# First propagation step of a four-layer graph network: two neighbouring pairs at once, with the operands swapped, against one pair at a time

## The chip, the cores and the metric

The kernel runs on one core of one Trainium2 chip, in one launch. The metric is the device time of that launch in microseconds (us). Everything is float32, and all four layers of the network, both steps of the last one included, are in this single program.

## The reference

Four layers work on 3327 nodes with 256 features each, every layer behind a layer norm and a ReLU, with a residual. Only the fourth is touched. In it `X` is the normed input, `S` the adjacency matrix, and two steps run, each with a sparse attention matrix `A` made from the current `Xa`:

```python
R = S + eye(N); R = R / R.sum(-1, keepdims=True)
Z, Xf, Xa = 0, X, X
for n in range(2):
    A  = top_p_attention(Xa, W1, W2, W3)   # softmax rows, cut to 90% of their mass
    Xf = R @ Xf                            # "propagation"
    Xa = A @ Xa
    Z  = Z + Xf @ U1[n].T + Xa @ U2[n].T
h = X + Z
x = x + layernorm(h)
```

What matters here is the first step's `R @ X`, a product of a 3327 x 3327 with a 3327 x 256 matrix, and what becomes of its result: it is multiplied by `U1[0].T` for `Z`, and it is the `Xf` of the second step.

## The kernel before

The nodes are 26 blocks of 128 rows (`T = 26`, `P = 128`); two blocks `p` and `p + 13` form a pair (`H = 13`). The product with `R` uses a scheme with seven products in place of eight on half matrices (numbers 1 to 7 in the code): sums of the adjacency's quarters, made in the third layer, lie in `s_dram`, and sums of the features' quarters in `ts`. So the first step costs 13 pairs x 7 products x 13 blocks of 128 x 128 x 128. `load_now` (L1255) loads a *slab*, 13 blocks of one product's adjacency operand (832 KB), through SP's queue into one of three buffers, and for four of the seven products GpSimd adds the identity to one block of it (L1264).

`PropagatedPair.steps` (L1272) issues the products: the slab's block is the stationary operand of TensorE, 128 feature columns are the moving one (L1295). A pair has two phases (`PHASES`: products 1, 2, 5, 4 and then 6, 7, 3; pair 0 has `FIRST_PHASES`). Their results collect in two PSUM banks; `half` (L1301) copies the first to SBUF on ScalarE, `whole` (L1306) adds the second in with VectorE. The results have nodes on the partitions.

`PropagationOfFirstStep` (L1356) then takes each block of 128 nodes: `scale` divides by the row sums on ScalarE, `turn` transposes the block with two TensorE transposes (L162, tile `pt_f`) and a ScalarE copy, and `sums` (L1372) multiplies by U1. It uses that the first step's share of `Z` can be folded into the second step: `sums` computes X U1[0] + Xf U1[1] with four matmuls of 256 columns (tiles `hT`, the turned input, loaded back from `hT_dram`, and `xT_f`), and this sum is what the second step multiplies by `R`. It is stored in `fs_dram` and read back as `fs` before the second step.

TensorE's order is written by hand (`manual_schedule(engines=PE_ALONE)`); the other engines' orders come from a scheduler. In the first step, row block `m` of the attention matrix goes through these stations: logits (L1063) and exponentials (L1088) three blocks ahead (`AHEAD = 3`), two ScalarE passes, then a search on VectorE that ends in the selection L1166; then TensorE turns the 26 blocks of the row (L202), ScalarE copies them (L205), and TensorE multiplies them by the features (L213). Between two row blocks TensorE runs one phase of a propagation (`propagate_first`), but for the row blocks in `APART = (3, 7, 11, 15, 19)`. The first `EARLY = 4` phases run before row block 0, the last three phases (`T - 3` to `T - 1`) follow row block 25 and lead to the second step. `plan` dictionaries say after which unit of a phase another piece of work (logits, `turn`, `sums`, `rows.begin` of the next row) is put into TensorE's order.

Of the kernel before, what the change touches and what calls it, by code (L numbers as in the profile page):

```python
# [11 lines left out]
F32 = mybir.dt.float32  # L12
# [35 lines left out]
def kernel(  # L48
# [73 lines left out]
    hT_dram = dram.tile([P, T, NC, P], F32, name="hT_dram")  # L122
    fs_dram = dram.tile([P, T, D], F32, name="fs_dram")
# [33 lines left out]

    def transposed(src, pool, name):

        pt = ps_tr.tile([P, 4, P], F32, tag="tr", name=f"pt_{name}")  # L160
        for c in range(NC):
            nc.tensor.transpose(pt[:, c, :], src[:, c * P : (c + 1) * P], ident)  # L162
        dst = pool.tile([P, NC, P], F32, tag="xT", name=f"xT_{name}")
        last_copied.append(nc.scalar.copy(dst, pt[:, :NC, :]))
        return dst
# [126 lines left out]
    def layers_0_to_2(again):  # L292
# [141 lines left out]
        class Pair:  # L434
# [27 lines left out]
            def turn(self):  # L462
                self.xT = turn_pair(self.xn, AF.Copy if self.layer == 3 else AF.Relu, *self.pool, self.name)
                if self.layer == 3:
                    for i in range(2):
                        nc.scalar.dma_start(hT_dram[:, self.p + i * H], self.xT[:, :, i * P : (i + 1) * P])
# [531 lines left out]
    def layer_3_in(again, tag, big, ep, w3, sm3, h3, kT0, ksum0, left):  # L998
# [16 lines left out]
        u1s = big.tile([P, 2, NC, D], F32, name="u1s")  # L1015
# [3 lines left out]
        def constants():  # L1019
            nc.scalar.dma_start(u1s, u1t.rearrange("s (c p) e -> p s c e", p=P))  # L1020
            for i in range(2):
                nc.scalar.dma_start(u2s[:, :, i, :], u2t[i].rearrange("(c p) e -> p c e", p=P))
# [69 lines left out]
        def search_steps(step, m, e, parts, st, dens, alone):  # L1092
# [49 lines left out]
            below, first, cand = s("below", 4), s("first"), s("cand", 8 * T)  # L1142
# [11 lines left out]
            for k in range(ROUNDS):  # L1154
                nc.vector.max(v[:, 8 * k : 8 * k + 8], cand)
                if k + 1 < ROUNDS:
                    left = s(f"cand{k % 2}", 8 * T)
                    nc.vector.match_replace(left, v[:, 8 * k : 8 * k + 8], cand, 0.0)
                    cand = left
# [51 lines left out]
        def propagated_steps(acc, step, m, xf):  # L1211
# [3 lines left out]
            for n, k in enumerate(order):  # L1215
                g, j = k // H, k % H
                if g not in slab:
                    s = slab[g] = slabs.tile([P, H, P], F32, tag="slab", name=f"slab3{tag}_{step}_{m}_{g}")
# [8 lines left out]
        FIRST_PHASES = (1, 2, 3), (5, 7, 4, 6)  # L1227
        PLACE3 = {2: (0, 0), 1: (0, 1), 4: (0, 2), 5: (0, 3), 6: (1, 0), 7: (1, 1), 3: (1, 2)}

        def combining(h, ts, a, b):  # L1230
# [5 lines left out]
            yield nc.vector.tensor_tensor(t3, part(1, 1), part(0, 1), ALU.subtract)  # L1236
            yield nc.vector.tensor_tensor(t2, part(1, 1), t1, ALU.subtract)
            yield nc.vector.tensor_tensor(t4, part(1, 0), t2, ALU.subtract)

        def combine(h, ts, a, b):  # L1240
            run(combining(h, ts, a, b))

        class PropagatedPair:


            def __init__(self, step, p, h, ts):
                self.step, self.p, self.h, self.ts = step, p, h, ts
                self.accs, self.slabs, self.name = {}, {}, f"{step}{tag}_{p}"
                self.last = step == 1 and p == H - 1

            def load(self, n):
                with tc.issue_after(slabs_behind[-1].ins) if slabs_behind else nullcontext():
                    self.load_now(n)

            def load_now(self, n):  # L1255
                p = self.p
                x = self.slabs[n] = slabs.tile([P, H, P], F32, tag="slab", name=f"slab3{tag}_{self.step}_{p}_{n}")
                if n in (1, 2, 4):
                    i, j = {1: (0, 0), 2: (0, 1), 4: (1, 1)}[n]
                    self.loaded = nc.sync.dma_start(x, adj_t[p + i * H, :, j * H : (j + 1) * H, :])  # L1260
                else:
                    self.loaded = nc.sync.dma_start(x, s_dram[:, p, {5: 0, 6: 1, 7: 2, 3: 3}[n]])
                if n in (1, 4, 5, 7):
                    added.append(nc.gpsimd.tensor_tensor(x[:, p, :], x[:, p, :], ident, ALU.add))  # L1264

            def right(self, n, k):
                if n in (1, 2, 3):
                    i, j = {1: (0, 0), 2: (1, 0), 3: (1, 1)}[n]
                    return self.h[:, i * H + k, j * P : (j + 1) * P]
                return self.ts[:, {5: 0, 6: 1, 7: 2, 4: 3}[n], k, :]  # L1270

            def steps(self, phase):  # L1272

                first = self.p == 0
                ns = (FIRST_PHASES if first else PHASES)[phase]
                units = [(n, k) for n in ns for k in range(H)]
                if first and not phase:
                    units.sort(key=lambda u: u[1] == H - 1)
                if first and not phase:
                    ends = w3.tile([P, 4, P], F32, tag="eT", name="ends", bufs=3)  # L1280
                    for i, n in enumerate(ns):
                        nc.sync.dma_start(ends[:, i, :], adj_t[0, :, n * H - 1, :] if n < 3 else s_dram[:, 0, 3, H - 1])
                place = {**PLACE3, 3: (2, 0)} if self.last else PLACE3
                last = {place[n][0]: (n, k) for n, k in units} if phase or not first else {}
                for at, (n, k) in enumerate(units):
# [6 lines left out]
                    a = self.slabs[n][:, k, :]  # L1292
                    if first and not phase and k == H - 1:
                        a = ends[:, ns.index(n), :]
                    nc.tensor.matmul(  # L1295
                        self.accs[bank][:, c * P : (c + 1) * P], a, self.right(n, k),
                        start=start, stop=last.get(bank) == (n, k), skip_group_check=True,
# [3 lines left out]
            def half(self):  # L1301
                self.y = w3.tile([P, 4, P], F32, tag="xf", name=f"xf_{self.name}")
# [53 lines left out]
        class PropagationOfFirstStep:  # L1356


            def __init__(self, m, rows):
                self.m, self.xf = m, rows  # L1360
                self.hT = w3.tile([P, NC, P], F32, tag="hT", name=f"hT_{m}")
                nc.sync.dma_start(self.hT, hT_dram[:, m])

            def scale(self, behind=last_turned):
                with tc.issue_after(behind[-1].ins):
                    nc.scalar.activation(self.xf, self.xf, AF.Copy, scale=rinv[:, self.m : self.m + 1])

            def turn(self):
                with tc.high_priority():
                    self.xT = transposed(self.xf, w3, f"f_{self.m}")  # L1370

            def sums(self):  # L1372
                acc = one_bank(f"u1_{self.m}")
                parts = [(xT[:, c, :], u1s[:, s, c, :]) for s, xT in enumerate((self.hT, self.xT)) for c in range(NC)]
                for i, (xT, u) in enumerate(parts):
                    nc.tensor.matmul(acc[:, :D], xT, u, start=(i == 0), stop=(i == len(parts) - 1))
                last = self.m % H == H - 1
                rows = fs[0][:, self.m, :] if last else self.hT.rearrange("p c n -> p (c n)")
                with tc.high_priority():
                    nc.scalar.copy(rows, acc[:, :D])  # L1380
                if not last:
                    nc.sync.dma_start(fs_dram[:, self.m, :], rows)

        def finish3(m, y, rows, name, behind=None):
# [3 lines left out]
            x3 = w3.tile([P, NC, P], F32, tag="hT", name=f"x3_{name}").rearrange("p c n -> p (c n)")  # L1388
            with tc.issue_after(behind.ins) if behind else nullcontext():
                nc.sync.dma_start(z, z_dram[:, m, :])  # L1390
                nc.sync.dma_start(x3, x3_dram[:, m, :])
# [26 lines left out]
        def finish_last(m, y, rows, acc, name, behind):  # L1418

            z = w3.tile([P, D], F32, tag="z", name=f"z1_{name}")  # L1420
            x3 = w3.tile([P, NC, P], F32, tag="hT", name=f"x3_{name}").rearrange("p c n -> p (c n)")
            with tc.issue_after(behind.ins):
                nc.sync.dma_start(z, z_dram[:, m, :])
                nc.sync.dma_start(x3, x3_dram[:, m, :])
# [18 lines left out]
        def finish_pair(p, both, pair):  # L1443
# [4 lines left out]
            zs, xs = [], []  # L1448
            for i in range(2):
                m = p + i * H  # L1450
                zs.append(w3.tile([P, D], F32, tag="z", name=f"z1_{m}"))
                xs.append(w3.tile([P, NC, P], F32, tag="hT", name=f"x3_{m}").rearrange("p c n -> p (c n)"))
                with tc.issue_after(pair.loaded.ins):
                    nc.sync.dma_start(zs[i], z_dram[:, m, :])
                    nc.sync.dma_start(xs[i], x3_dram[:, m, :])
                nc.gpsimd.tensor_tensor(zs[i], zs[i], ys.pop(m), ALU.add)
# [8 lines left out]
            for i in range(2):  # L1465
                z, x3, m = zs[i], xs[i], p + i * H
# [20 lines left out]
        def queries(step, m, name):  # L1487
            if step:
                return qT[:, m * P : (m + 1) * P]
            q = w3.tile([P, NC, P], F32, tag="xT", name=f"q_{name}")[:, 0, :]  # L1490
# [110 lines left out]
        APART = (3, 7, 11, 15, 19)  # L1601
# [4 lines left out]
        with tc.manual_schedule(engines=PE_ALONE):  # L1606
# [38 lines left out]
            pairs, fs = {}, []  # L1645

            def propagate_first(n, at):

                p, phase = divmod(n, 2)
                pair = pairs.setdefault(p, PropagatedPair(0, p, h3, ts))  # L1650
                units = H * len((PHASES if p else FIRST_PHASES)[phase])
                run(pair.steps(phase), {int(k * units // T): v for k, v in at.items()})
                if phase == (p == 0):
                    pair.half()
                if phase and n != T - 3 and n != T - 1:
                    rows_of_first(p)

            def rows_of_first(p):
                rows = pairs.pop(p).whole()
                for i in range(2):  # L1660
# [305 lines left out]
```

## Time and profile before

| | us |
|---|---|
| three timed runs, median (lowest to highest) | 2505.57 (2505.36 to 2507.46) |
| the profiled execution | 2506.95 |
| its span, first to last instruction | 2505.2 |
| TensorE busy in the span | 2484.1 (99%) |
| VectorE busy | 2093.6 (84%) |
| ScalarE busy | 1085.2 (43%) |
| GpSimd busy | 298.4 (12%) |

The first step of layer 3 lies between about 937 us (first propagation product) and 1781 us (first turning of the second step); the second step follows until the end. In the profile a float32 matmul shows as two records of TensorE, a transpose of a block as one. A line such as `L1295 PE MATMUL f0a<-h3a,slab3a 128*128 128x128 f32 x1008` names the program line, the engine, the operation, what is written from what, the stationary operand's size, the moving operand's size and type, and the number of records. In a timeline the first column is the start in us from the span's start, the second the length; the lengths of pipelined matmuls overlap, so the spacing of starts tells what one costs. Square brackets show how long the engine had been idle before, and what ended it. The granted clock of TensorE was 0.998 of full speed over the span.

### The profile page before, as it was taken

How to read it: one execution, taken by the hardware profiler on the slowest of the kernel's cores; microseconds unless marked ns; L12 is line 12 of the kernel's file. 1: busy time of each engine (PE TensorE's matmuls, PEld its weight loads, DVE VectorE, ACT ScalarE, POOL GpSimd, SP SyncE). 2: the span in 40 equal slices, each digit the busy share in tenths (PEclk: the TensorE clock that was granted, in tenths of full speed). 3: DMA queues.
4: the chain of work that ended last, by engine and by line, in shares of the span. 5: the costliest groups of instructions: out<-in, count | busy, mean ns of one | idle time of the engine just before them, and what ended most of it. 6: DMA issues, size and time to landing. Idle time of an engine off the chain costs nothing. (4 is left out here: it accounts for less than half of the span.)

```text
span 2505.2 us, 47792 instructions
## 1 busy us (share of the span) xinstructions
PE 2484.1 (99%) x17967; PEld 2256.5 (90%) x17967; DVE 2093.6 (84%) x5536; ACT 1085.2 (43%) x2158; POOL 298.4 (12%) x462
## 2 busy tenths in 40 slices
PE   9999999999999999999999999999999999999998
PEld 8999999999999998888888888888888888888887
DVE  7876789899887778788879797884999999999995
ACT  3101034443111115565656565653655655555551
POOL 2000010000000001000000000000121222322221
PEclk9999999999999999999999999999999999999999
DMA  6777766555798867323132323133433343344333
GB/s 201 228 232 240 225 192 185 174 178 177 240 315 285 281 210 227 96 81 108 58 121 80 110 85 106 57 108 113 164 122 109 109 138 121 109 129 140 124 110 114
DMA packets 181773, 388.28 MB, mean 155 GB/s; under 512 B 19741, under 2 KB 78746, under 8 KB 181530
## 3 DMA queue, kind: packets, MB, share of 16 engines
q1 hardware_dynamic: 153210, 364.31, 45.1%
q10 hardware_dynamic: 28320, 20.80, 2.6%
q8 instruction: 143, 2.34, 0.4%
q14 instruction: 100, 0.82, 0.1%
HBM read 315.44 MB, written 67.89 MB: 153 GB/s over the span
## 5 line engine op out<-in xcount | busy, mean ns | idle before, releaser
L205 ACT COPY eT_a<-pt_a 128x512 f32<-128x512 f32 (+1 forms) x364 | 196.4, 554 | 379.1 <-PE pt_a L202 376.7
L213 PE MATMUL a<-h3a,eT_a 128*128 128x256 f32 x1352 | 323.2, 382 | 0.0
L213 PE MATMUL a<-vs,eT_a 128*128 128x256 f32 x1352 | 320.3, 382 | 0.2 <-ACT eT_a L205 0.2
L1150 DVE MAX8 cand_a<-w 128x8 f32<-128x128 f32 x1352 | 288.4, 278 | 4.3
L213 PEld LDWEIGHTS a<-h3a,eT_a 128*128 128x128 f32 x1352 | 244.8, 190 | 33.3 <-ACT eT_a L205 2.1
L213 PEld LDWEIGHTS a<-vs,eT_a 128*128 128x128 f32 x1352 | 245.3, 191 | 29.9 <-ACT eT_a L205 0.7
L603 PE MATMUL acc_a<-tsa,s_a 128*128 128x128 f32 (+1 forms) x2028 | 269.9, 275 | 0.0
L603 PE MATMUL acc_a<-tsa,a_a 128*128 128x128 f32 x2028 | 251.6, 275 | 0.0
L603 PEld LDWEIGHTS acc_a<-tsa,s_a 128*128 128x128 f32 x2028 | 248.8, 192 | 0.7
L603 PE MATMUL acc_a<-rhs,a_a 128*128 128x128 f32 (+1 forms) x2028 | 248.6, 276 | 0.0
L603 PEld LDWEIGHTS acc_a<-tsa,a_a 128*128 128x128 f32 x2028 | 239.6, 192 | 0.5
L603 PEld LDWEIGHTS acc_a<-rhs,a_a 128*128 128x128 f32 x2028 | 236.7, 192 | 0.6
L1146 DVE SCALAR_TENSOR_TENSOR w<-e_a,t_a 128x896 f32<-128x896 f32 x208 | 225.5, 1084 | 3.0
L1264 POOL TENSOR_TENSOR slab3a<-slab3a,ident 128x128 f32<-128x128 f32 x100 | 114.3, 1143 | 912.6 <-DMA slab3a<-in_adj_t_dram 348.7
L202 PE MATMUL pt_a<-ident,e_a 128*128 128x128 f32 x1352 | 199.7, 274 | 3.0 <-DVE e_a L1166 2.8
L1088 ACT ACTIVATE e_a<-pl_a 128x1024 f32<-128x1024 f32 x260 | 184.5, 728 | 36.9 <-PE pl_a L1063 35.4
L202 PEld LDWEIGHTS pt_a<-ident,e_a 128*128 128x128 f32 x1352 | 166.2, 141 | 32.4 <-DVE e_a L1166 2.7
L1137 DVE SCALAR_TENSOR_TENSOR w<-e_a,t_a 128x3328 uint8<-128x3328 f32 x52 | 191.6, 3684 | 4.3
L1166 DVE SCALAR_TENSOR_TENSOR e_a<-e_a,all_least 128x3328 f32<-128x3328 f32 x52 | 191.9, 3690 | 1.8
L755 ACT ACTIVATE a_a<-a_a 128x640 f32<-128x640 f32 (+1 forms) x156 | 101.6, 666 | 163.0 <-DVE a_a L753 130.9
L420 ACT ACTIVATE xT_a<-pt_a 128x512 f32<-128x512 f32 x52 | 30.8, 593 | 321.1 <-PE pt_a L416 282.1
L1295 PE MATMUL f0a<-tsa,slab3a 128*128 128x128 f32 x1352 | 167.7, 276 | 0.0
(265 smaller groups left out, 4215.3 us busy)
## 6 DMA issues: line engine op xcount, KB each, us to landing
slab3a<-s_dram SPq DMA_DIRECT2D x100, 832.0 KB, 4.5
a_a<-in_adj_t_dram SPq DMA_DIRECT2D x312, 256.0 KB, 4.1
slab3a<-in_adj_t_dram SPq DMA_DIRECT2D x79, 832.0 KB, 4.6
a_a<-in_adj_t_dram SPq DMA_DIRECT2D x156, 320.0 KB, 4.0
s_dram<-s_a SPq DMA_DIRECT2D x78, 256.0 KB, 5.1
s_dram<-s_a SPq DMA_DIRECT2D x39, 320.0 KB, 4.5
x_dram<-x_a ACTq DMA_DIRECT2D x39, 256.0 KB, 3.7
s_dram<-a_a SPq DMA_DIRECT2D x26, 256.0 KB, 5.1
```

The lines of the kernel that those rows point to most:

```text
L202: nc.tensor.transpose(pt[:, j, :], e[:, k * P : (k + 1) * P], ident)
L205: last_turned.append(nc.scalar.copy(eT[:, : len(blocks), :], pt[:, : len(blocks), :]))
L213: nc.tensor.matmul(acc[:, :width], ready[g][:, j, :], rhs[:, k, :], start=(k == 0), stop=(k == T - 1))
L603: nc.tensor.matmul(self.acc[:, g, at : at + wide], quads[n][:, k - CUTS[c][0], :], t, start=(k == 0 and n in (1, 4)), stop=(k == H - 1 and ...
L755: nc.scalar.activation(a, a, AF.Tanh)
L1088: last_exp.append(nc.scalar.activation(dst, src, AF.Exp, accum_out=parts[:, c : c + 1]))
L1137: nc.vector.scalar_tensor_tensor(junk, e, t, e, ALU.is_lt, ALU.mult, accum_out=got)
L1146: nc.vector.scalar_tensor_tensor(w[:, : (b - a) * P], eg, t, eg, ALU.is_lt, ALU.mult, accum_out=below[:, g : g + 1])
L1150: nc.vector.max(cand[:, 8 * k : 8 * k + 8], w[:, (k - a) * P : (k - a + 1) * P])
L1166: nc.vector.scalar_tensor_tensor(e, e, least, e, ALU.is_ge, ALU.mult, accum_out=st["kept"][:, m : m + 1])
L1264: added.append(nc.gpsimd.tensor_tensor(x[:, p, :], x[:, p, :], ident, ALU.add))
L1295: nc.tensor.matmul(self.accs[bank][:, c * P : (c + 1) * P], a, self.right(n, k), start=start, stop=last.get(bank) == (n, k), skip_group_ch ...
```

## The change

The first step takes two neighbouring pairs, `p` and `p + 1`, at once (six doubles and one single pair 12), and the operands are swapped: 128 feature columns are stationary, and the blocks of both pairs' slabs, 256 columns, are moving. The results so come out turned, features on the partitions. The transposes, the scaling before them and `hT` go. The turned block is the stationary operand of one product with both U1[0] and U1[1] side by side (512 columns); the division by the row sums is done when that result is copied from PSUM. The half with U1[1] is read back as `fs` (so `fs` no longer holds the input's share), and the half with U1[0] is kept in `u_dram` and added to `z` by GpSimd in the second step. A double has four phases; its slabs come in pieces of 6 + 6 + 1 blocks per product, the last blocks of a phase's products sharing one buffer. The plans and `APART` are set anew.

```diff
-    hT_dram = dram.tile([P, T, NC, P], F32, name="hT_dram")
-    fs_dram = dram.tile([P, T, D], F32, name="fs_dram")
+    u_dram = dram.tile([P, T, 2, D], F32, name="u_dram")
...
+        OF_DOUBLE = (1, 2), (5, 4), (6, 3), (7,)
+        OF_LAST_DOUBLE = (1, 2), (5, 4), (6,), (3, 7)
+        OF_SINGLE = (1, 2, 5, 4), (6, 3, 7)
+        DOUBLES = H // 2
...
+        def load_slab(dst, n, p, q, a, b):
+            loaded = nc.sync.dma_start(dst, slab_source(n, p, q, a, b))
+            if n in (1, 4, 5, 7):
+                for t in range(p, q):
+                    if a <= t < b:
+                        x = dst[:, t - p, t - a, :]
+                        added.append(nc.gpsimd.tensor_tensor(x, x, ident, ALU.add))
+            return loaded
...
+        class FirstPropagation:
+            def __init__(self, d):
...
+                self.cuts = (0, H) if self.many == 1 else (0, 6, 12, H)
...
+            def units(self, phase):
+                units = [(n, k) for n in self.phases[phase] for k in range(H)]
+                if self.many > 1:
+                    units.sort(key=lambda u: u[1] == H - 1)
+                return units
+            def steps(self, phase):
...
+                for at, (n, k) in enumerate(units):
+                    c = sum(k >= b for b in self.cuts[1:-1])
+                    if (n, c) not in self.slabs:
+                        self.load(phase, n, c)
+                    nc.tensor.matmul(
+                        self.acc[:, self.at[n]], right_half(h3, ts, n, k), self.slabs[n, c][:, :, k - self.cuts[c], :],
+                        start=not at, stop=at == len(units) - 1, skip_group_check=True,
+                    )
+                    yield at
+            def keep(self, phase):
...
+                        nc.scalar.copy(
+                            y, self.acc[:, k * width : (k + 2) * width].rearrange("p (n f) -> p n f", n=2)
+                        )
...
+                        if n == 6:
+                            nc.vector.tensor_tensor(y0[:, 0:1, :], y0[:, 0:1, :], y0[:, 1:2, :], ALU.add)
+                            nc.vector.tensor_tensor(y0[:, 1:2, :], y0[:, 1:2, :], b, ALU.add)
+                            nc.vector.tensor_tensor(y1, y1, both(y0[:, 1:2, :]), ALU.add)
+                        elif n == 3:
+                            nc.vector.tensor_tensor(y0[:, 1:2, :], y1[:, 1:2, :], b, ALU.add)
+                        else:
+                            nc.vector.tensor_tensor(y1, y1, both(b), ALU.add)
...
         class PropagationOfFirstStep:
-            def __init__(self, m, rows):
-                self.m, self.xf = m, rows
-                self.hT = w3.tile([P, NC, P], F32, tag="hT", name=f"hT_{m}")
-                nc.sync.dma_start(self.hT, hT_dram[:, m])
-            def scale(self, behind=last_turned):
-                with tc.issue_after(behind[-1].ins):
-                    nc.scalar.activation(self.xf, self.xf, AF.Copy, scale=rinv[:, self.m : self.m + 1])
-            def turn(self):
-                with tc.high_priority():
-                    self.xT = transposed(self.xf, w3, f"f_{self.m}")
+            def __init__(self, m, yT):
+                self.m, self.yT = m, yT
             def sums(self):
-                acc = one_bank(f"u1_{self.m}")
-                parts = [(xT[:, c, :], u1s[:, s, c, :]) for s, xT in enumerate((self.hT, self.xT)) for c in range(NC)]
-                for i, (xT, u) in enumerate(parts):
-                    nc.tensor.matmul(acc[:, :D], xT, u, start=(i == 0), stop=(i == len(parts) - 1))
+                m, acc = self.m, one_bank(f"u1_{self.m}")
+                for c in range(NC):
+                    nc.tensor.matmul(
+                        acc, self.yT[:, c, :], u1s[:, c].rearrange("p s e -> p (s e)"),
+                        start=(c == 0), stop=(c == NC - 1),
+                    )
+                rows = w3.tile([P, 2, D], F32, tag="rows", name=f"u1_{m}", bufs=1)
...
+                        nc.scalar.activation(rows.rearrange("p s e -> p (s e)"), acc, AF.Copy, scale=by)
...
+                    nc.sync.dma_start(u_dram[:, m], rows)
...
         def finish3(m, y, rows, name, behind=None, of_pair=None):
...
+            nc.gpsimd.tensor_tensor(z, z, u, ALU.add)
             nc.gpsimd.tensor_tensor(z, z, y, ALU.add)
...
-        APART = (3, 7, 11, 15, 19)
+        APART = (2, 6, 11, 16, 21)
...
-                    propagate_first(0, dict(zip((23, 25.4), ([what] for what in left.stages))))
+                    propagate_first(0, dict(zip((15, 18, 19, 22), ([what] for what in (*left.stages, sum_keys, centre_keys)))))
...
-                    steps = prepare(0, 0, kT0)
-                    centred = {7.5: [lambda: centre(kT0, mean0(), "0"), lambda: next(sums_of_first)]}
-                    propagate_first(1, merged(centred, whole_run(steps, 14.5), plan))
+                    propagate_first(1, merged(whole_run(prepare(0, 0, kT0), 3), {12: [lambda: next(sums_of_first)]}))
...
-                    steps = prepare(0, m + AHEAD, kT0)
-                    after = {3: [a.turn], 15: [a.node], 18: [a.values], 20: [lambda: rows.begin(m + 1)]}
-                    propagate_first(next(propagated), merged(whole_run(steps, 10), after, later))
+                    steps, n = prepare(0, m + AHEAD, kT0), next(propagated)
+                    at = (4, 14, 18, 22, 24) if n % 4 == 3 else (3, 10, 15, 18, 20)
+                    what = a.turn, lambda: next(steps), a.node, a.values, lambda: rows.begin(m + 1)
+                    propagate_first(n, merged(dict(zip(at, ([x] for x in what))), later))
...
-                    nc.scalar.dma_start(fs[0][:, a:b, :], fs_dram[:, a:b, :])
+                    nc.scalar.dma_start(fs[0][:, a:b, :], u_dram[:, a:b, 1, :])
```

## The prediction

> **What bounds the kernel now.** I read four views in this order: the page's totals, the busy time by window over the first step, the chain of waits filtered to TensorE, and the timeline of TensorE's starts.
>
> ```profile
> PE 2484.1 (99%) x17967; PEld 2256.5 (90%) x17967; DVE 2093.6 (84%) x5536; ACT 1085.2 (43%) x2158; POOL 298.4 (12%) x462
> ...
> 1050.00:1200.00 150.00, 149.96 (x938) 125.98 (x939) 123.20 (x364) 91.22 (x188) 11.66 (x18) 1.00 0.30 96
> ...
> PE pt_a L202 <- DVE e_a L1166: 2.8, 2, 2.5
> ...
> 936.93 8.05 PE L1295 MATMUL f0a<-h3a,slab3a 128*128 128x128 f32 x70 [0.34 <-issue]
> 944.82 0.60 PE L416 MATMUL pt_a<-ident,h3a 128*128 128x128 f32 x4
> ...
> 995.39 1.97 PE L202 MATMUL pt_a<-ident,e_a 128*128 128x128 f32 x8 [2.49 <-DVE e_a L1166]
> ```
>
> TensorE is the bound: 149.96 of 150 us in the stretch from 1050 (columns: PE, PEld, DVE, ACT, POOL, then the clock, 1.00). In the changed stretch (937 to 1781) it waits for a selection only twice, 2.8 us together. So each record taken out of it is worth its *spacing*, if nothing else becomes late. A length (276 ns) is not the price, since lengths overlap; spacings of starts are:
>
> ```profile
> 971.36 0.38 PE L162 MATMUL pt_f<-ident,xf_0a 128*128 128x128 f32 x2
> ...
> 971.58 3.29 PE L1295 MATMUL f0a<-tsa,slab3a 128*128 128x128 f32 x28
> ...
> 1012.27 1.03 PE L1376 MATMUL u<-u1s,xT_f 128*128 128x256 f32 x4
> 1013.14 1.72 PE L1295 MATMUL f0a<-h3a,slab3a 128*128 128x128 f32 x14
> ...
> 1025.26 1.88 PE L1346 MATMUL u<-u2s,xT_a 128*128 128x512 f32 x4
> 1026.97 1.05 PE L1295 MATMUL f0a<-tsa,slab3a 128*128 128x128 f32 x8
> ```
>
> 936.93 to 944.82 is 7.89 us for 70 records of 128 columns: 112.7 ns. A transpose record takes 0.22 / 2 = 109 ns, one of 256 columns 0.87 / 4 = 216 ns, one of 512 columns 1.71 / 4 = 430 ns.
>
> **The change part by part.**
>
> *Products.* Before, 13 pairs x 7 x 13 = 1183 products of two records. After, the single pair keeps 91 of them (its operands swap, its sizes don't), and the doubles make 546 products of 256 columns where there were 1092 of 128. Each gives 4 x 112.7 - 2 x 216.3 = 18.3 ns: 546 x 18.3 = 10.0 us. The weight loads halve, but they lie beside the matmuls.
>
> Here a rule speaks against the change. By the rows a narrow record costs 112.7 and a wide one 216. The Trainium skill, "TensorE: Matmul & The Clock Gate", section "Back-to-back issue gap", gives an isolated gap of N/2.4 + 2.5 ns. The 512-column row (430 ns) says that a float32 record passes twice over its columns; so the rule makes 109.2 and 215.8, and the doubling would save only 2 x 2.5 = 5 ns, 2.7 us in all. The 256-column row agrees, the 128-column one lies 3.5 ns above. The same section says that at small N the formula leaves out the weight load, which fits. The trace decides: 10.0; by the rule the sum below would be 7.3 smaller.
>
> *Transposes* `pt_f`: 52 records x 109 ns = 5.7 us, gone.
>
> *Sums with U1.* 26 x 8 records of 216 become 26 x 4 of 430: 44.9 against 44.7, so 0.2. TensorE's work falls by 15.9 us.
>
> *Nothing on the path.* ScalarE loses 26 `scale` and 26 copies (43% busy, cover everywhere). The loads of `hT` and the stores of `hT_dram` go. The keeping of results goes from four or five small operations per pair to as many wide ones per double; VectorE (635.8 of 785.6 us busy from row 0 to the second step) moves about the same elements, so zero. GpSimd gets 26 more adds `z + u` and SP's queue 26 loads of 128 KB: in the second step the add `z + y` is done about 15 us before VectorE takes `z`, and some 6 us before at the last row, against about 0.7 per add; zero, and 0.7 us at the tail if that cover were gone. The `u_dram` stores stand on SP's queue, where the next slab's load can queue behind a store that waits for ScalarE's copy; I take zero, up to 1 us.
>
> *The early phases (936.93 to 995.39) take on new waits.* Pieces of 6 blocks are half as long as a slab of 13 before, but each serves two pairs, and the new order asks for `ts` and keys earlier.
>
> ```profile
> 943.23 1.89 DVE L1235 TENSOR_TENSOR tsa<-h3a 128x1664 f32<-128x1664 f32 x1
> ...
> 951.19 2.24 DVE L1043 TENSOR_SCALAR kT_0a<-kT_0a,kmean_0a 64x1664 f32<-64x1664 f32 x2
> ...
> 967.05 3.76 POOL L1264 TENSOR_TENSOR slab3a<-slab3a,ident 128x128 f32<-128x128 f32 x1 [6.38 <-PE pl_a L1063]
> ...
> 966.81 3.69 DVE L1137 SCALAR_TENSOR_TENSOR w<-e_a,t_a 128x3328 uint8<-128x3328 f32 x1
> ...
> L1264 POOL TENSOR_TENSOR slab3a<-slab3a,ident x100: 452/498/3862, 745.7 to 2474.5; 128x128 f32<-128x128 f32 x100
> ...
> slab3a<-s_dram SPq DMA_DIRECT2D x100, 832.0 KB, 4.5
> ```
>
> The last two are the identity adds (min/median/max ns) and the slabs' loads (KB, us to landing). The mean of the keys and their centring stand in VectorE's queue between the sums `ts`; by the start times above TensorE will wait about 1.1 us for the key mean and 0.4 for the centred keys. A slab piece has about 3.5 us between the release of its buffer and its use in phase 0; it needs 4.5 to land and, for products 1, 4, 5 and 7, two adds in series. By the order of the four products in question I get 0.85 (no add), 1.1 and 2.6 us (with adds) of waiting. Sum 6.05 us, against 2.5 now (the 2.49 at 995.39): row 0's search then runs as freely as the second step's first one, which takes 35.8 us from its logits (row 0 now: 41.2); from 953.6 that is ready at about 989, before TensorE asks for it. Net cost 3.5 us.
>
> A second rule bears on the two adds. The row: one add beside an L1137 pass took 3.76 us, exactly as long as that pass; the median is 0.498. The Trainium skill, "GPSIMD Engine Reference", section "1. Specifications", says that its SBUF interfaces are shared with VectorE and contend with VectorE instructions that have two SBUF inputs. By the rule, with VectorE at 84%, most double adds would fall under such passes: about 4.3 us each in place of 1.0. By the row's median they don't. I take the median, and keep the rule for the rival below: two or three more tiles caught would cost 6 to 10 us.
>
> *The middle.* Spare time between a selection and its first turning is 2.5 us at the tightest (rows 8 and 16), 5 to 16 otherwise. `APART` moves to rows that follow long phases (four phases per double are longer than two per pair), so I see no new wait there. Two places are tight:
>
> ```profile
> 1708.61 3.68 DVE L1166 SCALAR_TENSOR_TENSOR e_a<-e_a,all_least 128x3328 f32<-128x3328 f32 x1
> ...
> 1717.37 1.04 PE L202 MATMUL pt_a<-ident,e_a 128*128 128x128 f32 x8
> ```
>
> The last row (25) has 5.1 us to spare now (selection 1712.3, turned 1717.4). After, TensorE has only about 72.4 us of work between the turnings of rows 22 and 25, against three searches on VectorE of 24.5 us (the last now: selections 1687.8 and 1712.3) and some 1 us of keeping between them: about 2 us of waiting. And at the change from phase `T - 3` to `T - 2` the single pair's slab of product 1 is asked for 3.4 us ahead against 4.5 and an add: about 2 us. The second step's first row waits 0.34 us now (1780.87) and should not: its search takes 35.8 us from its logits, over which TensorE has about 41 us of work. The reload of `fs` lands in 9.4 us at the median and is needed about 11 us after its last issue; its packets halve to 1 KB, so up to 2 us, taken as zero.
>
> *Sum*: -15.9 + 3.5 + 2 + 2 - 0.5 = about -9 us. The profiled execution is 2506.95 (span 2505.2 and 1.75 around it), 1.4 above the median 2505.57; so a profiled one of about 2498 and a median of 2496.5.
>
> **The rivals.** About 0.2% (5 us, so 2500.6 and 2510.6) is what a measurement can tell from no change.
>
> *A, the sum*: 2496.5, its own range 2493 to 2500.5. Chance 0.45.
>
> *B, no new wait lasts.* For it: the DMA share is only 0.30 in the middle, so loads may land faster in half-size pieces, and the early waits are worked out from 1 us margins. All 15.9 less about 1: 2490. Chance 0.24.
>
> *C, slabs become the bound (slower).* One mechanism: a double's tile lands late, because its pieces give shorter runs of bytes (3 KB and 512 B against 6.6 KB), six pieces share three buffers, and its two adds stand under VectorE's passes. In the trace of before TensorE never waits for a slab, which speaks against it; but the lead shrinks to 3.5 us at five phase boundaries that follow each other with no row block between (0 to 3, and `T - 3` to `T - 1`), and to about 9 us within phases. It decides from about 7 us of landing and adding: five boundaries x 4 us and a few in-phase waits outweigh 15.9, for about 2515. Chance 0.09.
>
> *D, the swap doesn't narrow.* If a moving operand of two separated blocks costs as two of 128 (225 ns per record), the 10.0 goes: 2506.5. No row before has such an operand; the upper bound is this, the lower the 216 of a contiguous one, and I take 216 as the nearest row by size. Chance 0.08.
>
> *E, the search chain.* TensorE's work per row falls by about 0.4 us while VectorE's (24 to 25 us per row) doesn't. If a wide keeping operation falls before each selection, VectorE's lateness is handed to TensorE once per double: six or seven waits of 1 us, about 2502. For: 84% busy; against: 5 to 16 us of slack. Chance 0.14.
>
> **How the numbers follow.** Faster by over 0.2%: A and B but for their tails, and a quarter of E, 0.70. Within: most of E, D, and A's upper tail, 0.20. Slower: C and a little of D, 0.10. The range 2488 to 2504 holds A, B and E, 0.8.
>
> **What would show it.** Right: starts of the product's records 216 ns apart, no `pt_f`, 16 us less busy spacing between 937 and 1781, new idle time on TensorE before products in the first 60 us (about 6 us, released by loads, GpSimd adds and VectorE's centring) and about 4 us near row 25 and phase `T - 2`. Wrong: records 225 ns apart (D); TensorE waiting for the slab in many phases, or a landing above 7 us (C); waits for the selection L1164 in more than two rows (E); none of these and a gain of 15 (B).

## The result

The changed kernel takes 2498.01 us (median of 8 runs, 2496.63 to 2503.98) against 2505.74 us for the kernel before (8 runs, 2502.67 to 2509.01). The ratio is 0.997, with a 95% interval of 0.9959 to 0.9981: 4.8 to 10.3 us less, by the medians 7.7. Measured once more beside other kernels the ratio was 0.9972 (0.9963 to 0.9981). The forecast was 2496.5, with a range of 2488 to 2504.

The profiled execution is 2498.93 us, its span 2497.0. First the page's totals of the kernel after, then the waits of TensorE from 930 on (engine and line, what it waited for: us in total, times, longest; 0.3 us ahead of the first product left out):

```profile
PE 2471.1 (99%) x16719; PEld 2187.2 (88%) x16719; DVE 2094.2 (84%) x5506; ACT 1075.8 (43%) x2109; POOL 287.6 (12%) x488
```

```profile
PE a L215 <- ACT eT_a L207: 3.4, 11, 0.4
PE f0a L1308 <- POOL slab3a_0a L1258: 2.5, 3, 1.7
PE pt_a L204 <- DVE e_a L1164: 1.4, 1, 1.4
PE f0a L1308 <- DMA slab3a_0a<-s_dram: 1.3, 1, 1.3
PE f0a L1308 <- DMA slab3a_0a<-in_adj_t_dram: 1.1, 1, 1.1
PE pk_mean_0a L1028 <- DVE ktotal_0a L1032: 0.5, 1, 0.5
```

VectorE is as busy as it was, ScalarE about 9 us less; TensorE is still the bound. But where it waited 2.8 us before for selections, and 0.7 us for ScalarE, it now waits some 10 us, in six ways. Five of them are in the prediction; the first row, which had 0.2 us before, is not.

The timeline of TensorE in the kernel after, early phases, row block 0 and the end of phase `T - 3`:

```profile
947.17 1.54 PE L1308 MATMUL f0a<-slab3a_0a,h3a 128*128 128x256 f32 x6
949.01 0.70 PE L1308 MATMUL f0a<-slab3a_0a,tsa 128*128 128x256 f32 x2 [0.30 <-POOL slab3a_0a L1258]
950.21 1.56 PE L1308 MATMUL f0a<-slab3a_0a,tsa 128*128 128x256 f32 x6 [0.49 <-POOL slab3a_0a L1258]
...
966.00 1.99 PE L1308 MATMUL f0a<-slab3a_0a,tsa 128*128 128x256 f32 x8 [1.31 <-DMA slab3a_0a<-s_dram]
...
982.42 1.13 PE L1308 MATMUL f0a<-slab3a_0a,tsa 128*128 128x256 f32 x4 [1.74 <-POOL slab3a_0a L1258]
...
991.33 0.93 PE L204 MATMUL pt_a<-ident,e_a 128*128 128x128 f32 x7
...
1739.70 1.49 PE L1308 MATMUL f0a<-slab3a_0a,h3a 128*128 128x128 f32 x11 [1.07 <-DMA slab3a_0a<-in_adj_t_dram]
```

Slabs or their adds end a wait at each of the three phase boundaries of the first double, and again where the single pair begins. Row block 0 no longer waits for its selection (no bracket at 991.33). A bracket counts from the end of the work before it, and lengths overlap; by spacing (gap less 216 ns) the five early delays are 0.69 (key mean), 0.46, 0.66, 1.47 and 1.90, together 5.2 us.

Single executions differ by some 3 us already in layers 0 to 2, which the change doesn't touch: the first product starts at 936.93 and 934.06 in two executions of the kernel before, at 934.93 and 933.24 in two of the kernel after. So I compare stages. Times are from the timelines, each number the difference of two starts; "row 0" is the first turning of row block 0, "second" that of the second step:

| us | first product to row 0 | row 0 to second | second to end | first product to end |
|---|---|---|---|---|
| before | 58.5 | 785.5 | 724.3 | 1568.2 |
| before, again | 58.5 | 786.2 | 725.1 | 1569.8 |
| after | 56.4 | 782.1 | 723.6 | 1562.1 |
| after, again | 56.3 | 782.1 | 723.8 | 1562.2 |

By stages the gain is 6.0 to 7.7 us, depending on which executions are paired: about 2 before row 0, 3.4 to 4.1 in the middle, 0.5 to 1.5 in the second step. Three things have to be known to read the columns.

Work has moved between the first two: the sums with U1 of two blocks (16 records of 216 ns, 3.5 us) and their turnings stood ahead of row 0 in the kernel before, and those sums stand behind it now.

Row 0's wait cost more than its 2.5 us. After it the clock granted to TensorE was half of full speed for 3.4 us, in both executions of the kernel before (0.50, the third column from the end); the changed kernel keeps 1.00 at this place. First the kernel before, then after:

```profile
994.95:998.35 3.40, 2.96 (x11) 2.56 (x12) 3.40 (x18) 1.17 (x2) 0.30 (x1) 0.50 0.66 246
991.40:994.80 3.40, 3.16 (x21) 2.66 (x20) 3.26 (x6) 1.07 (x2) 0.94 (x2) 1.00 0.92 323
```

From its first turning to the turning of its 25th block, row 0 took 13.0 and 13.7 us in the two executions before, 11.9 in both after: 1.1 and 1.7 us that went together with the wait. They are also why the two executions before differ by 0.7 in the middle.

The third column contains the time after TensorE's last record, 9.6 and 10.5 us in the two executions before, 10.4 and 10.5 after (from the start of that record). Without it the second step takes 714.7 us in both before and 713.3 in both after: 1.4 less, all of it in the step's first row. There 0.4 are four turnings, and 0.6 is the gap of a wait for exponentials on ScalarE that the kernel before had ahead of one of them (840 ns between two starts in place of 216); the rest is spread over smaller gaps. The wait in the kernel before:

```profile
1803.63 0.44 PE L162 MATMUL pt_f<-ident,xf_0a 128*128 128x128 f32 x2 [0.46 <-ACT e_a L1088]
```

From the first product to TensorE's last record the gain is 6.9 us between the first two executions and 7.6 between the repeats. These repeat runs had been announced so:

> The kernel before, profiled once more. If the 2.0 us by which its first product started later than the changed kernel's (936.93 against 934.93) is scatter, it starts now somewhere from 932 to 937, and from there to the end it takes 1568 us again. If it is part of the change (other loads in flight), it starts again near 937.

> The changed kernel once more, beside the others: 7 to 8 us below the kernel before if the first result stands. From its first product to the end its profiled execution should again take 1562 us; the time ahead of that, which the change doesn't touch, may differ by 2 us either way if that is only scatter between executions.

The start ahead of the change is scatter, then. (One execution of the kernel before took 2505.69 us; the second measurement of the changed kernel had a median of 2500.13 against 2507.84.)

### The profile page after: what moved, and what is told of

The parts are those of the page before. It is cut to its first block, busy times and chain, and to the rows that moved or that the text cites. A ratio compares the mean times of both kernels' runs of the same rounds, so it can differ in the third digit from the quotient of the medians.

```text
span 2497.0 us, 45220 instructions
## 1 busy us (share of the span) xinstructions
PE 2471.1 (99%) x16719; PEld 2187.2 (88%) x16719; DVE 2094.2 (84%) x5506; ACT 1075.8 (43%) x2109; POOL 287.6 (12%) x488
## 5 line engine op out<-in xcount | busy, mean ns | idle before, releaser
L1308 PE MATMUL f0a<-slab3a_0a,tsa 128*128 128x256 f32 (+1 forms) x728 | 163.2, 368 | 3.8 <-POOL slab3a_0a L1258 2.5
L1120 ACT ACTIVATE junk_a<-e_a,t_a 128x3328 uint8<-128x3328 f32 x52 | 159.8, 3073 | 1.0 <-POOL parts_a L1082 0.6
```

The costliest lines, as they stand in the source:

```text
L1120: nc.scalar.activation(junk_a, e, AF.Relu, scale=-1.0, bias=t, accum_out=short)
L1308: nc.tensor.matmul(self.acc[:, self.at[n]], right_half(h3, ts, n, k), self.slabs[n, c][:, :, k - self.cuts[c], :], start=not at, stop=at = ...
```

## The experiments

**What the doubling is worth (split).** The two columns of blocks are multiplied one after the other:

```diff
-                    nc.tensor.matmul(
-                        self.acc[:, self.at[n]], right_half(h3, ts, n, k), self.slabs[n, c][:, :, k - self.cuts[c], :],
+                    for t in range(self.many):
+                        x = self.at[n]
+                        nc.tensor.matmul(
+                            self.acc[:, x.start + t * P : x.start + (t + 1) * P], right_half(h3, ts, n, k),
+                            self.slabs[n, c][:, t, k - self.cuts[c], :],
```

> The changed kernel, but each product of 256 columns is issued as two of 128 with the same stationary operand; slabs, sums, plans are untouched. Theory (spacing by the trace): 546 x 18.3 ns = 10.0 us more work on TensorE; the early phases and the last ones get longer, so 1 to 3 us of the waits for slabs and for row 25's selection go. Against the changed kernel +7 to +10 us, so about 2505 to 2508, as slow as before. Rival (isolated gap of the rule): the doubling is worth 2.7 us at most, so at most 2501, and the gain came from elsewhere.

Measured: 2506.94 us, ratio to the kernel before 1.0001 (0.9993 to 1.0009); from the first product to the end 1570.0, 7.9 us more than the changed kernel (7.8 more than its repeat). The whole gain is gone, so the rule's 2.7 us is out. But it need not be 10.0 either. In the split kernel's timeline:

```profile
1045.95 3.29 PE L1310 MATMUL f0a<-slab3a_0a,tsa 128*128 128x128 f32 x28
1049.17 3.07 PE L1062 MATMUL pl_a<-kT_0a,qT 64*128 64x512 f32 x16
```

and in the changed kernel's:

```profile
974.48 5.34 PE L1308 MATMUL f0a<-slab3a_0a,h3a 128*128 128x256 f32 x24
979.66 0.60 PE L1308 MATMUL f0a<-slab3a_0a,tsa 128*128 128x256 f32 x2
```

24 wide records in 5.18 us are 216 ns each. The 28 narrow ones in 3.22 us seem to be 115, but the gap to the logits is longer than one between two products. Over all gaps between neighbouring product records, the few with a pause in them left out, a narrow one is 111.6 ns (4294 gaps of the kernel before, 2195 of the split one), a wide one 215.95 (933 gaps of the changed one). So a doubled product saves 4 x 111.6 - 2 x 215.95 = 14.5 ns, and 546 of them 7.9 us. The split kernel gives back as much up to the end; up to TensorE's last record it is 8.7, with about 1.1 us more of waits before row 0 (58.9 us, of which the products explain 1.3).

**What the turning is worth (turns).** Two transposes per block are put back on TensorE alone, ahead of the product that overwrites them:

```diff
                 m, acc = self.m, one_bank(f"u1_{self.m}")
                 for c in range(NC):
+                    nc.tensor.transpose(acc[:, c * P : (c + 1) * P], self.yT[:, c, :], ident)
+                for c in range(NC):
                     nc.tensor.matmul(
```

> The changed kernel with two transposes of the block ahead of each product with U1, written to the bank that the product then overwrites, read by nobody: TensorE's share of the turning is put back, without its copy and scaling. Theory: 52 records x 109 ns = 5.7 us, all on the path: about 2503.7. Rival: part of it falls into time in which TensorE waits anyway (row 25, the second step's first row has 6 us to spare only on VectorE's side), then 3 to 4 us.

Measured: 2504.86 us, ratio 0.9998 (0.999 to 1.0006); 1568.6 us from the first product to the end, 6.5 more than the changed kernel, and 5.7 more between row 0 and the second step. 48 of the 52 records lie in that stage, 5.2 us by their spacing, and the other four add 0.4 to TensorE's second step: the turning cost its whole price, nothing of it was hidden. Before row 0, where nothing was edited, this execution took 57.1 us against 56.4: its slab waits were longer, so a single execution can be off by 0.7 there.

**Who makes TensorE wait for the turned row (sums_later).** Five of the eleven waits in the first row, the longest ones, are new. The changed kernel in a row block without a propagation behind it, ScalarE and TensorE in one timeline:

```profile
1068.94 1.88 PE L1439 MATMUL u<-u1s,y_0a 128*128 128x512 f32 x4
1070.76 3.07 PE L1062 MATMUL pl_a<-kT_0a,qT 64*128 64x512 f32 x16
1071.93 1.02 ACT L1087 ACTIVATE e_a<-pl_a 128x1024 f32<-128x1024 f32 x1 [0.38 <-PE pl_a L1062]
...
1075.59 1.03 PE L204 MATMUL pt_a<-ident,e_a 128*128 128x128 f32 x8
...
1076.46 1.03 PE L215 MATMUL a<-h3a,eT_a 128*128 128x256 f32 x4
...
1077.26 1.05 ACT L207 COPY eT_a<-pt_a 128x512 f32<-128x512 f32 x2
1077.88 2.00 PE L215 MATMUL a<-h3a,eT_a 128*128 128x256 f32 x8 [0.39 <-ACT eT_a L207]
```

The next row is turned at 1075.59, but its copy stands on ScalarE behind the exponentials of the logits just issued and the small operations that follow them, and runs at 1077.26. TensorE has one group of matmuls left to fill that time with, and then stands still for 0.56 us (a gap of 772 ns in place of 216, in each of the five rows of `APART`). In the kernel before the same moment was covered:

```profile
1106.32 3.07 PE L1063 MATMUL pl_a<-kT_0a,qT 64*128 64x512 f32 x16
...
1111.15 1.02 PE L1376 MATMUL u<-u1s,hT 128*128 128x256 f32 x4
1112.01 1.03 PE L1376 MATMUL u<-u1s,xT_f 128*128 128x256 f32 x4
1112.87 1.04 PE L202 MATMUL pt_a<-ident,e_a 128*128 128x128 f32 x8
1113.75 2.76 PE L213 MATMUL a<-h3a,eT_a 128*128 128x256 f32 x12
```

There the product with U1 came after the logits, and the next row's first products follow its turnings without a wait; the change puts the product ahead of the logits. The edit puts it behind the next row's first turnings, in these rows alone:

```diff
-                if props:
+                if props and not (not interleaved and m != T - 3 and m + 1 < T):
                     plan = merged(plan, {4: [props.pop(0).sums]})
...
                     plan = merged(plan, {5: [lambda: rows.begin(m + 1)]})
+                    if props:
+                        plan = merged(plan, {5: [props.pop(0).sums]})
```

> The changed kernel, but in the row blocks without a propagation behind them the product with U1 is put after the next row's first turnings, not ahead of the logits. In the trace TensorE there waits about 0.55 us for ScalarE's first copy of the turned row, which stands behind the exponentials, in each of 5 rows. Theory: 5 x 0.55 = 2.8 us less, about 2495.2, and the product with U1 covers the copy. Rival: the wait only moves (the copy is late by the exponentials all the same): no change.

Measured: 2493.97 us, ratio to the kernel before 0.9948 (0.9935 to 0.9961); row 0 to the second step 778.9, 3.1 us less than the changed kernel, the rest of the way unchanged. In its timeline the product now stands where the wait was:

```profile
1072.25 1.03 PE L204 MATMUL pt_a<-ident,e_a 128*128 128x128 f32 x8
...
1073.12 1.88 PE L1439 MATMUL u<-u1s,y_0a 128*128 128x512 f32 x4
...
1073.92 1.05 ACT L207 COPY eT_a<-pt_a 128x512 f32<-128x512 f32 x2
1074.84 2.75 PE L215 MATMUL a<-h3a,eT_a 128*128 128x256 f32 x12
```

**Lead or landing (ends_inside).** A double's tile of 12 blocks leaves the thirteenth of its buffer free. Here the last block of each pair lies in it, and the shared tile of last blocks, which held a whole buffer for 0.9 us of work, is gone:

```diff
-                self.cuts = (0, H) if self.many == 1 else (0, 6, 12, H)
+                self.cuts = (0, H) if self.many == 1 else (0, 6, 12)
...
+                        self.slabs[n, c, "end"] = x[:, H - 1 :, :]
+                        end = self.slabs[n, c, "end"].rearrange("p (t k) m -> p t k m", t=1)
+                        load_slab(end, n, self.p + c, self.p + c + 1, H - 1, H)
...
+                    (n, k, c) for n in self.phases[phase] for c in range(2) for k in (*range(6 * c, 6 * c + 6), H - 1)
```

> The changed kernel, but the last block of a product (column 12 of each of the two pairs) lies in the free thirteenth block of the slab tile of 12, as two products of 128 columns, and the tile that a phase's last blocks shared is gone. A tile then is asked for two tiles (5.6 us) ahead of its use everywhere, against 3.45 at a phase's boundary. Theory: the waits for slabs and their adds at the boundaries (0.46 + 0.66 at 948, 1.47 at 964, 1.90 at 980, 1.1 at 1738) go, up to 5.6 us; 84 more records of 128 for 42 wide ones cost 0.8, and row 0's search may hold back 1 us: about -3.5, so 2494.5. Rival: landing, not the lead, sets these waits, or row 0's selection takes their place: 0 to -1.

Measured: 2495.94 us, ratio 0.9956 (0.9943 to 0.9969); row 0 to the second step 1.4 us less than the changed kernel, first product to row 0 about the same (56.4). All waits for slabs and adds are gone from TensorE's list, also at the single pair, so a longer lead removes them. But the first phase now needs the last pair of `h3` after 12 records, which is when VectorE is still making it. The waits of this kernel:

```profile
PE f0a L1314 <- DVE h3a L462: 3.5, 1, 3.5
PE a L215 <- ACT eT_a L207: 2.5, 7, 0.4
PE pt_a L204 <- DVE e_a L1164: 1.4, 1, 1.4
```

And the stretch after the longest of them:

```profile
941.60:944.95 3.35, 3.35 (x10) 2.64 (x9) 3.35 (x3) 0.00 (x0) 0.00 (x0) 0.50 0.73 245
```

Again the granted clock is 0.50 for 3.4 us, and most products there start 427 ns apart. The wait and this stretch cost 3.7 + 1.8 us, about what the early waits had cost (5.2): that is why the first stage is as long as before the edit. I had looked only at the slabs; the order of the changed kernel, last blocks at the end of the phase, also hid the end of the layer before.

**What the adds are of it (no_adds).** The identity is left out of the first double's slabs (and with it the order that put the next keys' tile behind the last of these adds):

```diff
-            if n in (1, 4, 5, 7):
+            if n in (1, 4, 5, 7) and diagonal:
```

> The changed kernel without the identity on the diagonal blocks of the first double's slabs (left out of the computation there). Theory: the waits at 948 and 980 are landing plus two adds of 0.43 us; without the adds TensorE still waits for the landing: 1 to 2 us less than the changed kernel, about 2496.5. Rival (adds locked out by VectorE's passes, as the rule has it): the adds are all of these waits, 3 us less, about 2495. If the lead has nothing to do with it, the DMA wait at 964 goes as well.

Measured: 2497.92 us, ratio 0.9965 (0.9952 to 0.9978), which the changed kernel's interval doesn't exclude. The stages say more: first product to row 0 is 55.2 us, 1.1 to 1.2 less, the others the same. The waits at 949 and 950 are gone, the one at 982 is down to 1.08, the one at 966 stays:

```profile
966.23 1.99 PE L1308 MATMUL f0a<-slab3a_0a,tsa 128*128 128x256 f32 x8 [1.25 <-DMA slab3a_0a<-s_dram]
...
982.00 1.13 PE L1308 MATMUL f0a<-slab3a_0a,tsa 128*128 128x256 f32 x4 [1.08 <-DMA slab3a_0a<-s_dram]
```

By spacing 1.1 us went at the first boundary and 0.7 at 982. So 1 to 2 us of the early delays are adds (one execution, in a stage that can be off by 0.7), the larger part is landing against a short lead.

**Both edits, the first phase left alone (both_first).** The edits of sums_later and ends_inside, but phase 0 of the first double as in the changed kernel:

```diff
+                if not self.d and not phase:
+                    return [
+                        (n, k, k // 6) for a, b in ((0, H - 1), (H - 1, H)) for n in self.phases[phase] for k in range(a, b)
+                    ]
```

> Both earlier edits together (product with U1 after the next row's first turnings; last blocks in the free thirteenth block of their tiles), except in the very first phase, which keeps the shared tile of last blocks: there the earlier edit made TensorE wait 3.5 us for the last pair of h3. Theory: the gains add: 3.1 (rows apart) and 1.4 (row 0 to second step), and in the early phases the waits at 964 and 980 (3.4) go while those at 948 (1.1) stay: together about 7 us below the changed kernel, about 2491. Rival: row 0's selection, which had 3.9 us to spare, takes over in the early phases: 5 us below.

Measured: 2489.48 us (5 runs, 2488.89 to 2492.11), ratio to the kernel before 0.9933 (0.9919 to 0.9946), 16.8 us by the ratio and 18.4 by the medians; this beats both kernels. From the first product to the end it takes 1554.6 us, 7.4 less than the changed kernel: 2.2 before row 0, 4.8 from there to the second step. Its waits:

```profile
PE f0a L1321 <- POOL slab3a_0a L1258: 1.7, 3, 0.9
PE pt_a L204 <- DVE e_a L1164: 1.4, 1, 1.4
PE pk_mean_0a L1028 <- DVE ktotal_0a L1032: 0.5, 1, 0.5
PE a L215 <- ACT eT_a L207: 0.5, 2, 0.2
```

The wait at 966 went; the one at 982 shrank from 1.74 to 0.93 and is one for an add, so the lead alone doesn't remove it. Row 0's selection still had 1.2 us to spare.

## Why the prediction was right, and where its sum was off

- *Direction and size*: -9 forecast, -7.7 by the medians, -6.0 to -7.7 by the stages. It is case A, the sum.
- *Products, -10.0*: the mechanism held, the term was 2.1 us too large. It measured 7.9. I had divided one stretch of 70 records by its length, and a pause in that stretch (its first gap is 185 ns) went into the 112.7. Since the term is a difference of two nearly equal numbers, 1 ns per narrow record moved it by 2 us. The rule's 2.7 was further off: the wide record is at its 215.8, but the narrow one lies 2.4 ns above its 109.2.
- *Transposes, -5.7*: confirmed by the turns run. *Sums, -0.2*: records at about 430 ns, as forecast.
- *Early waits, 6.05, less the 2.5 of row 0*: 5.2, at the places named (key mean, three boundaries; the one for the centred keys did not come), and the wait for row 0's selection went. What the prediction missed is the half clock after that wait: with it, row 0 gave 3.7 to 4.4 us, not 2.5. The two adds took 0.86 us at 982, as the median had it, and 1.94 at 948. Pairs of 3 us and more occurred only where the lead was long; the one at 1508.68 took 3.72 us beside a VectorE pass of 3.69 (the add of the prediction was near its pass in length, 3.76 against 3.69, not equal). So the rule on the shared interfaces fits the trace, but it did not decide the time.
- *Row 25, 2, and phase `T - 3` to `T - 2`, 2*: the waits are there, by spacing 1.6 (selection) and 1.2 us (slab). *The second step's first row* no longer waits (no bracket at its first turning, 6.2 us after its selection), as forecast.
- *"I see no new wait there" (the middle)*: this step failed. I checked `APART` against the selections alone and not against the copies on ScalarE, and charged nothing for moving the product with U1 ahead of the logits. It cost 2.8 us in five gaps, and moving it back gave 3.1.
- *Nothing on the path*: TensorE's second step is 1.4 us shorter, not equal. The added `z + u` and loads cost nothing there, and a wait ahead of a turning, which the prediction did not count, is gone with the turning.
- *Sum with the measured terms* (waits by spacing): -7.9 - 5.7 - 0.2 + (5.2 - 2.7) + 1.6 + 1.2 - 0.5 + 2.8 = -6.2, where 2.7 and 0.5 are the waits ahead of row 0 and of the second step's first row in the kernel before. The half clock (-1.1 and -1.7) and the wait ahead of the turning (-0.6) make it -7.9 and -8.5, against the -6.9 and -7.6 measured to TensorE's last record. The 1 us left over lies in smaller gaps that were not taken apart. So the size came out close partly by luck: 2.1 us too much for the products and 2.8 us of waits not seen made the forecast too good, while waits taken 2 us too long and two savings not seen worked the other way.
- *Rivals*: B is out (the waits came). C is out: the tiles land as fast as the slabs before. D is out: a moving operand in two pieces costs 215.95 ns, the price of a contiguous one (216). E is out: one row waits for its selection, not six. The landings (KB each, median us):

```profile
slab3a_0a<-s_dram SPq DMA_DIRECT2D x48, 768.0 KB, 4.7
slab3a_0a<-in_adj_t_dram SPq DMA_DIRECT2D x36, 768.0 KB, 4.5
```

## What to carry to other kernels

When the bound engine is 99% busy, every removed record counts at its spacing, but take the spacing from the middle of all gaps, not from one stretch: a saving that is a small difference of two large costs carries the error in full. A wait of that engine can be worth more than its length: look at the granted clock behind it. When a piece of work on the bound engine is moved, ask what it covered where it stood, on every engine that feeds the next step; here a product between the logits and the next row had covered ScalarE's exponentials and what follows them. With a ring of buffers, a small tile costs as much lead as a large one: put it into free room of its neighbours, and look at what else its old place hid.

## What the runs showed that I had not expected

In three executions TensorE had a wait of 2.49 to 3.50 us behind the first product (both of the kernel before, and the one of ends_inside), and in each the granted clock was then 0.50 for 3.4 us. In the seven others, whose waits there were at most 2.1 us, it was not, up to TensorE's last record. What lies between the two lengths was not tried.

Two executions of one kernel agree within 0.1 us from the first product to row 0 and within 0.7 from there to the second step (within 0.1 in the changed kernel, which has no such stretch), while their starts differ by up to 2.9 us (936.93 and 934.06). A difference of 3 us in the first step can be read from two profiles, though the medians of five to fourteen runs leave an interval of about 0.1% to either side. And a pair of adds by GpSimd took between 0.86 and 3.72 us in the same kernel, those of 3 us and more where nothing waited for them.
